# Two graph layers on one core: the bias add on another engine, and loads and stores at other places of a hand-ordered program

## The chip, the core and the metric

The kernel runs on one core of one Trainium2 chip. TensorE does the matrix products. VectorE (DVE), ScalarE (ACT) and GpSimd (POOL) work beside it. One queue, that of SyncE (SP), issues nearly all transfers between HBM and SBUF. The metric is the device time of one execution in microseconds (us).

## The reference, cut to what matters

```python
# x: 16 batches of 1024 x 128; adj: 1024 x 1024; all fp32
h = relu(layernorm(x))
x = x + (adj @ (h @ W0) + bias0)              # layer 0
h = relu(layernorm(x))
def step(h):                                  # layer 1: five steps
    m = adj @ h                               # in_matrix and out_matrix are both adj
    av = concatenate([m, m], axis=-1)
    u3 = h @ u3_w.T + u3_b
    z = sigmoid(av @ w3_w.T + w3_b + u3)
    r = sigmoid(av @ w4_w.T + w4_b + u3)
    hv = tanh(av @ w5_w.T + w5_b + (r * h) @ u5_w.T + u5_b)
    return (1 - z) * h + z * hv
x = x + step(step(step(step(step(h)))))
```

## The kernel before, in words

**Quads and stages.** The 16 batches are worked on in four quads of four. Layer 0's product with the adjacency matrix is done plainly for quads 0 and 1 (`aggregate_plainly`, L535; the trace calls its sums `pq_a`), and in layer 1's way for quads 2 and 3. While the plain products run, VectorE also makes sums of adjacency blocks (`right_sums`, L240), which are stored to HBM as `rd` and later streamed back.

**Layer 1.** Quads 0 and 1 take their steps in turn, then quads 2 and 3: (0,0), (1,0), (0,1), (1,1) and so on, where (q,n) is step n of quad q. The very last is (3,4). A step has two parts. In the *aggregation* (`aggregate`, L436) 49 small products of 256-blocks (7 x 7, a two-level scheme with fewer products than 8 x 8) give `mT`, adjacency times state. In the *gates* (`gates`, L711), first for the pair of batches A and then for the pair B, TensorE multiplies with the gate weights and VectorE updates the state `hT_all`.

**A product.** `multiply(i, p)` (L486) takes a left operand made by VectorE (`big`, `little`) and a right operand that is either resident or one of 12 slots of `ring`. ScalarE copies the result out of PSUM into `Z` or `taps`. After p = 3 and p = 4 VectorE adds these up (`Z<-Z,taps`), and after p = 4 it also adds a level into `mT`, for i = 4 three adds one after the other. After every second streamed product, `stream()` (L294) issues the load of a 512 KB pair that is used some ten products later (`ring<-rd`).

**Places.** What else is to be done is hung on places: `put(k, piece)` (L620) notes it, and `place(k)` (L623) runs the pieces of k. In an aggregation place k comes right after product k - 1. In the plain products there is a place every four matmuls. In the gates the places have names: `Ar0`-`Ar3`, `Az0`-`Az3`, `Br0`-`Bz3`. Each engine, and SP's queue, runs its own work in program order. A wait at the head of a queue holds all behind it.

**The pieces that matter here.**

- `bias(b)` (L647) adds layer 0's bias in place to the x tile of batch b, 128 partitions by 8 x 128 fp32. GpSimd does it. For quads 0 and 1 it stands at places of the two plain products, and for the others in `put_statistics` (L678), at 23 and 37 of a step.
- `TRANSPOSED` (L88): in the steps (1,0), (1,4) and (3,0) the four parked batches of a quad are loaded as 32 x 32 squares (`sqt<-ft`, `transposing`, L603) and turned by VectorE into `hT_all` (L613), two transposes each.
- After its gates each batch is turned back into squares (`squares_to_dram`, L576; `sq`) and stored (`fn<-sq`), for the next step to load in natural layout (`nat<-fn`).
- `output(b)` (L627) has three pieces: loads of `ho` (four transfers of 128 KB) and of `x1d` (512 KB), the add, and the store.
- The squares, `sqt`, `ho`, and the normalised batches `ha` and `hb` (written by `relu` of `put_statistics`) all share one pool `flip` of three buffers (L118). The tiles of x share a pool `pre` of four (L117).
- `po` (L651) multiplies by layer 0's weights and adds to x. Its PSUM bank comes from a pool of four, which the plain sums use as well (L123).

Of the kernel before, what the change touches and what calls it, by code (L numbers as in the profile page):

```python
# [93 lines left out]
def tile_two_gnn_layers(  # L94
# [9 lines left out]
    nc = tc.nc  # L104
    pin = tc.keep_in_program_order
# [6 lines left out]
    Q = 4  # L112
    quads = B // Q
# [11 lines left out]
    def dma(out, in_):  # L125
        pin(nc.sync.dma_start(out=out, in_=in_))

    def by_slots(ap):
        return ap.rearrange("(p c) d -> p c d", c=NC)

    def x_tile(b):
        return pre.tile([P, NC, D], F32, tag="xt", name=f"xt_{b}")

    def load_x(b, xt=None, parts=((0, NC),)):
        xt = xt if xt is not None else x_tile(b)
        for cs in parts:
            cs = slice(*cs)
            dma(xt[:, cs], by_slots(x[b])[:, cs])
        return xt
# [39 lines left out]
    xts = {0: load_x(0, parts=((0, 2), (2, CH), (CH, NC)))}  # L179
# [57 lines left out]
    def add(o, a, b):  # L237
        pin(nc.vector.tensor_add(o, a, b))  # L238
# [194 lines left out]
    def period(i):  # L433
        return 2 + 7 * i
# [132 lines left out]
    def flip_tile(nm):  # L567
        return flip.tile([P, NSQ, NC, SQ], F32, tag="sq", name=nm)
# [16 lines left out]
    def natural_from(blocks, hN):  # L585

        for k in range(NSQ):
            dma(by_blocks(hN, k), blocks[k])
# [31 lines left out]
    def put(k, *pieces):  # L620
        fixed.setdefault(k, []).extend(pieces)
# [5 lines left out]
    def output(b, blocks):  # L627
        box = {}

        def load():  # L630
            box["h"] = flip_tile(f"ho_{b}")
            natural_from(blocks, box["h"])
            box["x1"] = x_tile(f"1_{b}")
            dma(box["x1"], x1s[b])

        def rest():
            x1 = box["x1"].rearrange("p j (a e) -> p a j e", e=SQ)
            for g in range(NH):
                js = bass.ts(g, CH)
                add(x1[:, :, js], x1[:, :, js], box["h"][:, :, js])  # L640

        def store():
            dma(by_slots(out[b]), box["x1"])

        return load, rest, store

    def bias(b):  # L647
        both = gb.unsqueeze(1).to_broadcast([P, NC, D])
        pin(nc.gpsimd.tensor_add(xts[b], xts[b], both))

    def po(b, g):  # L651
        pt = ps_g.tile([P, CH, D], F32, tag="pg", name=f"po_{b}_{g}")
# [25 lines left out]
    def put_statistics(kind, first):  # L678

        rest = []  # L680
        for n, b in enumerate((first, first + 1)):
            box = {}

            def begin(b=b, box=box):
                box["n"] = Norm(xts[b], None, f"{kind}{b}")
                box["n"].statistics(range(CH))

            def relu(k, b=b, box=box):
                def run():
                    if k == 0:  # L690
                        box["n"].dst = flip_tile(f"h{kind}_{b}")
                    box["n"].relu(range(2 * k, 2 * k + 2))

                return run

            def done(b=b, box=box):
                (keep if kind == "a" else layer_1_input)(b, box["n"].dst)

            key = "AB"[n]
            put(f"{key}r3", begin)  # L700
            put(f"{key}z1", lambda box=box: box["n"].statistics(range(CH, NC)))
            put(f"{key}z3", lambda box=box: box["n"].scales(EVERY))
            rest.append((10, lambda box=box: box["n"].shift(EVERY)))
            rest += [(11 + 13 * n + 3 * k, relu(k)) for k in range(CH)]
            rest.append((22 + 14 * n, done))
            if kind == "a":
                rest.append((23 + 14 * n, lambda b=b: bias(b)))
        return rest


# [73 lines left out]
    def loads_of_next(source, places):  # L784

        for k, at in enumerate(places):
            put(at, lambda k=k: natural_from(source[k], nat[:, k]))

    def step(i, loads_at=(period(4), period(5), "Ar0", "Ar2"), early_places=GATE_PLACES):
        st = state[i]  # L790
        quad, n = st["quad"], st["step"]
        nm = f"{quad}_{n}"
        hT = [hT_all[:, i, k] for k in range(Q)]
        last = n == STEPS - 1
        final = last and quad == quads - 1
        other = state[1 - i]
        me = (quad, n)
        for k, piece in relus.pop("next", ()):
            put(k, piece)
        for b, k in LOADS.get(me, ()):  # L800
            put(k, lambda b=b: xts.update({b: load_x(b)}))
        if me in TRANSPOSED:
            q = TRANSPOSED[me]
            for k in range(Q):
                load, turn_it = transposing(q * Q + k, hT_all[:, q % 2, k])
                put((12, 16, 26, 30)[k], load)
                put((24, 28, 36, 40)[k], turn_it)
        if me in OUTPUTS:
            for k, piece in zip((16, 34, 38), outputs[OUTPUTS[me]]):
                put(k, piece)  # L810
        block = BLOCKS.get(me)

        source = h0_of(block) if block else other["blocks"]
        if final:
            st["x1"] = []

            def load_x1(k):
                x1 = x_tile(f"1_{quad * Q + k}")
                dma(x1, x1s[quad * Q + k])
                st["x1"].append(x1)  # L820

            for k in range(Q):
                for piece, at in zip(outputs[(quad - 1) * Q + k], (0, 13, 16)):
                    put(4 + 9 * k + at, piece)
            for k, at in enumerate((32, 42, "Ar0", "Ar3")):
                put(at, lambda k=k: load_x1(k))
        if source is not None:
            loads_of_next(source, loads_at)
        aggregate(nm, place)
        if me in NORMS:  # L830
            relus["next"] = put_statistics(*NORMS[me])
        if source is not None:
            for k, piece in zip(early_places, early_pieces(made[0])):
                put(k, piece)
        stored, ready = {}, {}

        def turn(first):
            def run(k):
                k += first
                stored[k] = Later(lambda n: ready[k][n])  # L840

                def squares():
                    store, ready[k] = squares_to_dram(hT[k], f"{nm}_{k}")
                    if k == Q - 1:
                        put(9, store)
                    else:
                        store()

                if k == Q - 1:
                    put(3, squares)  # L850
                else:
                    squares()

            return run

        for a, key in enumerate("AB"):
            pair = slice(2 * a, 2 * a + 2)
            if final and a == 1:
                for k, (load, rest) in enumerate(final_outputs(quad, st, stored)):
                    put(f"Br{2 * k}", load)  # L860
                    put(f"Bz{2 * k + 1}", rest)
            gates(
                [mT[:, 2 * a + k] for k in range(2)],
                hT[pair],
                f"{nm}{key}",
                key,
                turn(2 * a),
                finish=finish(quad, hT[pair], st) if final and a == 1 else None,
            )
        if final:  # L870
            st["quad"], st["blocks"] = None, None
            return
        st["step"] += 1
        st["blocks"] = [stored[k] for k in range(Q)]
        if last:
            outputs.update({quad * Q + k: output(quad * Q + k, stored[k]) for k in range(Q)})
            begin(i, quad + 2)
        if block:
            loads_of_next(other["blocks"], (period(3) + 4, period(4) + 4, period(5) + 2, period(6)))
            pieces = early_pieces(made[0] + 1)  # L880
            for k, piece in zip(BLOCK_PLACES, pieces):
                put(k, piece)
            aggregate(f"a{block}", place)
            for k in range(Q):
                for g in range(NH):
                    po(block * Q + k, g)
                    if 2 * k + g in (1, 2, 6, 7):
                        pieces[{1: 6, 2: 7, 6: 8, 7: 9}[2 * k + g]]()

    outputs = {}  # L890
# [21 lines left out]
    def h0_of(quad):  # L912
        return Later(lambda k: h0_blocks[quad * Q + k])
# [105 lines left out]
            (lambda: early(2 * Q - 1)) if b == Q else None,  # L1019
        )  # L1020
    for b in range(Q):
        put(9 + b // 2, lambda b=b: bias(b))
    for k in (3, 7, 8, 9, 10, 11, 12, 13, 14, 15):
        sums_at(k, 1)
    for b in range(Q):
# [39 lines left out]
    for k in range(Q):  # L1065
        b = Q + k
# [56 lines left out]
```

## Time and profile before

| what | value |
|---|---|
| time, median of 3 runs (lowest to highest) | 1807.7 us (1807.47 to 1808.23) |
| the profiled execution's own time | 1806.57 us |
| its span, first to last instruction | 1804.8 us |
| TensorE busy | 1774.4 us, 98% |
| VectorE busy | 1373.6 us, 76% |
| ScalarE busy | 900.1 us, 50% |
| GpSimd busy | 95.2 us, 5% |
| the 16 DMA engines, queue of SP | 68.4% |
| mean granted TensorE clock | 0.998 |

A row of a timeline gives the start in us, the duration, the engine, the line, what is written from what, the number of instructions merged, and in brackets how long the engine sat idle before and what ended that. A row of waits gives who waited for whom: us in total, times, longest.

### The profile page before, as it was taken

Reading aid. Unit: us, or ns where it says so; the run is one execution under the profiler, and the core shown is the slowest. Engines: PE = TensorE matmul, PEld = TensorE weight load, DVE = VectorE, ACT = ScalarE, POOL = GpSimd, SP = SyncE. Lnnn points to the kernel's source line nnn. Section 1 sums busy time; section 2 is a strip of 40 time slices with the busy share of each in tenths; the row PEclk is TensorE's granted clock in tenths of the full one; section 3 lists DMA queues with packets and bytes.
Section 4 is the critical chain, followed back from the end, with each engine's and each line's share of the span. In section 5 each row is a group of like instructions: output and inputs, shape, how many; then the busy total and the mean of one; then the engine's idle time right before and its main releaser. Section 6 shows DMA issues by size and latency. Waiting matters only on the chain.

```text
span 1804.8 us, 21485 instructions
## 1 busy us (share of the span) xinstructions
PE 1774.4 (98%) x6466; PEld 1208.6 (67%) x6466; DVE 1373.6 (76%) x2777; ACT 900.1 (50%) x1969; POOL 95.2 (5%) x57
## 2 busy tenths in 40 slices
PE   9999989999999999999999999999999999999998
PEld 4458576678685766758857667585766857667574
DVE  5758889677788697877787968777687777867776
ACT  5236555554555555644355554445445454444544
POOL 3331010100000001100000000000000000000000
PEclk9999999999999999999999999999999999999999
DMA  6298784759675957648849476594856749477493
GB/s 219 88 365 291 215 306 151 223 191 256 183 251 179 301 177 223 204 158 270 251 131 332 158 246 243 177 271 150 279 177 208 244 149 303 147 230 236 138 347 119
DMA packets 168866, 396.36 MB, mean 220 GB/s; under 512 B 18480, under 2 KB 86960, under 8 KB 168752
## 3 DMA queue, kind: packets, MB, share of 16 engines
q1 hardware_dynamic: 168752, 395.00, 68.4%
q8 instruction: 52, 0.85, 0.2%
q14 instruction: 62, 0.51, 0.1%
HBM read 314.18 MB, written 80.74 MB: 219 GB/s over the span
## 4 chain that ended last, share of the span: by engine, by line
PE 88%; DMA 5%; DVE 4%; issue 1%; POOL 1%; SPq 0%; ACT 0%; POOLq 0%; DVEq 0%; ACTq 0%
PE a L500 24%; PE c L500 12%; PE b L500 6%; PE pq_a L543 4%; PE a_a L500 3%; DMA ring<-rd 2%; PE pr_3B L720 2%; PE pr_2B L720 2%; PE pr_1B L720 2%; PE pr_4A L720 2%; PE pr_2A L720 2%; PE pr_1A L720 2%; PE pr_0A L720 2%; PE pr_3A L720 2%; PE pr_0B L720 2%; PE pr_4B L720 2%
## 5 line engine op out<-in xcount | busy, mean ns | idle before, releaser
L500 PE MATMUL a<-ring,big 128*128 128x256 f32 x1120 | 288.2, 380 | 4.4 <-DMA ring<-rd 4.4
L519 ACT COPY Z<-a 128x256 f32<-128x256 f32 x480 | 177.0, 371 | 209.1 <-PE a L500 202.7
L238 DVE TENSOR_TENSOR Z<-Z,taps 128x512 f32<-128x512 f32 (+1 forms) x264 | 157.5, 603 | 151.1 <-ACT taps L519 150.9
L500 PE MATMUL c<-ring,little 128*128 128x256 f32 x960 | 246.9, 380 | 5.5 <-ACT taps L519 3.3
L500 PEld LDWEIGHTS a<-ring,big 128*128 128x128 f32 x1120 | 212.8, 191 | 41.5 <-issue 11.8
L238 DVE TENSOR_TENSOR mT<-mT,Z 128x1024 f32<-128x1024 f32 x154 | 186.7, 1224 | 39.9 <-ACT Z L519 34.9
L500 PEld LDWEIGHTS c<-ring,little 128*128 128x128 f32 x960 | 182.4, 190 | 31.4 <-ACT taps L519 4.1
L519 ACT COPY taps<-c 128x256 f32<-128x256 f32 x280 | 103.6, 370 | 120.1 <-PE c L500 114.6
L500 PE MATMUL a<-ring,little 128*128 128x256 f32 x560 | 146.0, 384 | 6.5 <-DVE little L235 6.5
L500 PE MATMUL b<-ring,big 128*128 128x256 f32 x560 | 143.8, 380 | 0.0
L500 PE MATMUL a<-resident,little 128*128 128x256 f32 x560 | 143.8, 380 | 0.0
L500 PEld LDWEIGHTS a<-ring,little 128*128 128x128 f32 x560 | 105.6, 191 | 24.7 <-ACT taps L519 8.4
L500 PEld LDWEIGHTS b<-ring,big 128*128 128x128 f32 x560 | 106.7, 190 | 14.2
L500 PEld LDWEIGHTS a<-resident,little 128*128 128x128 f32 x560 | 106.7, 190 | 14.2
L581 DVE STREAM_TRANSPOSE sq<-hT_all 128x512 f32<-128x512 f32 x156 | 101.2, 687 | 0.0
L398 ACT COPY big<-nat 128x512 f32<-128x512 f32 x132 | 80.6, 614 | 0.0
L519 ACT COPY taps<-b 128x256 f32<-128x256 f32 x140 | 52.0, 371 | 55.5 <-PE b L500 55.0
L235 DVE TENSOR_TENSOR little<-little,big 128x256 f32<-128x256 f32 x154 | 65.4, 425 | 7.1 <-DVE little L238 0.5
L238 DVE TENSOR_TENSOR little<-big 128x256 f32<-128x256 f32 x154 | 64.2, 417 | 0.7 <-ACT big L398 0.7
L235 DVE TENSOR_TENSOR little<-big 128x256 f32<-128x256 f32 x154 | 64.2, 417 | 0.0
L235 DVE TENSOR_TENSOR little<-big,little 128x256 f32<-128x256 f32 x154 | 64.1, 416 | 0.0
L341 POOL TENSOR_TENSOR rstd_b<-ve_b,mhalf 128x8 f32<-128x8 f32 x16 | 27.5, 1717 | 550.0 <-DVE ve_b L340 536.6
(250 smaller groups left out, 2946.6 us busy)
## 6 DMA issues: line engine op xcount, KB each, us to landing
ring<-rd SPq DMA_DIRECT2D x440, 512.0 KB, 6.0
fn<-sq SPq DMA_DIRECT2D x78, 512.0 KB, 2.8
nat<-fn SPq DMA_DIRECT2D x256, 128.0 KB, 6.8
x1d<-xt SPq DMA_DIRECT2D x16, 512.0 KB, 5.6
sqt<-ft SPq DMA_DIRECT2D x16, 512.0 KB, 7.1
xt<-x1d SPq DMA_DIRECT2D x16, 512.0 KB, 7.0
xt<-in_x_dram SPq DMA_DIRECT2D x15, 512.0 KB, 5.3
ho<-fn SPq DMA_DIRECT2D x56, 128.0 KB, 6.3
```

Of the source, the lines that this page charges most:

```text
L235: pin(nc.vector.tensor_sub(o, a, b))
L238: pin(nc.vector.tensor_add(o, a, b))
L341: pin(nc.gpsimd.tensor_tensor(self.rstd[:, part], self.ve[:, part], mhalf[:, part], ALU.pow))
L398: return [lambda i=i: pin(nc.scalar.copy(made_of(k, i), part(a, b, i))) for i in range(2)]
L500: nc.tensor.matmul(bank, l, right[:, c, :], start=opens and c == 0, stop=c == SB - 1, skip_group_check=True,)
L519: pin(nc.scalar.copy(to, bank))
L543: nc.tensor.matmul(bank, hN[i][:, c, :], raw[c // SB][g][:, c % SB], start=c == 0, stop=c == NC - 1,)
L581: pin(nc.vector.transpose(squares_of_half(sq, g), transposed_half(hT, g)))
L720: nc.tensor.matmul(bank, w_sb[:, w, :], moving, start=start, stop=stop, skip_group_check=True)
```

## The change

Five edits:

1. VectorE does layer 0's bias add in place of GpSimd, and it stands at other places: 7 to 10 of the first plain product (before 9, 9, 10, 10), and 26 and 36 of a step (before 23 and 37). In the second plain product its places 6, 8, 10, 12 stay.
2. The parked batches of `TRANSPOSED` are loaded at 8, 18, 28, 38 and turned at 17, 27, 37, 47 (before 12, 16, 26, 30 and 24, 28, 36, 40).
3. The store of the squares of batch 2 of each quad is issued at place 4 of the next aggregation (before at once, in the gates). That of batch 3 stays at 9.
4. The pieces of the outputs of quad 2 in the last step stand earlier, and the first of them is loaded in step (2,4), at `Bz1`.
5. Of the four loads of the last quad's own x, the first two stand at 17 and 34 (before 32 and 42).

```diff
--- before.py
+++ after.py
@@ -646,7 +646,7 @@
 
     def bias(b):
         both = gb.unsqueeze(1).to_broadcast([P, NC, D])
-        pin(nc.gpsimd.tensor_add(xts[b], xts[b], both))
+        add(xts[b], xts[b], both)
 
     def po(b, g):
         pt = ps_g.tile([P, CH, D], F32, tag="pg", name=f"po_{b}_{g}")
@@ -704,7 +704,7 @@
             rest += [(11 + 13 * n + 3 * k, relu(k)) for k in range(CH)]
             rest.append((22 + 14 * n, done))
             if kind == "a":
-                rest.append((23 + 14 * n, lambda b=b: bias(b)))
+                rest.append((26 + 10 * n, lambda b=b: bias(b)))
         return rest
 
 
@@ -803,8 +803,8 @@
             q = TRANSPOSED[me]
             for k in range(Q):
                 load, turn_it = transposing(q * Q + k, hT_all[:, q % 2, k])
-                put((12, 16, 26, 30)[k], load)
-                put((24, 28, 36, 40)[k], turn_it)
+                put(8 + 10 * k, load)
+                put(17 + 10 * k, turn_it)
         if me in OUTPUTS:
             for k, piece in zip((16, 34, 38), outputs[OUTPUTS[me]]):
                 put(k, piece)
@@ -819,10 +819,11 @@
                 dma(x1, x1s[quad * Q + k])
                 st["x1"].append(x1)
 
-            for k in range(Q):
-                for piece, at in zip(outputs[(quad - 1) * Q + k], (0, 13, 16)):
-                    put(4 + 9 * k + at, piece)
-            for k, at in enumerate((32, 42, "Ar0", "Ar3")):
+            for k, places in enumerate(((None, 10, 13), (2, 18, 21), (15, 28, 31), (24, 40, 43))):
+                for piece, at in zip(outputs[(quad - 1) * Q + k], places):
+                    if at is not None:
+                        put(at, piece)
+            for k, at in enumerate((17, 34, "Ar0", "Ar3")):
                 put(at, lambda k=k: load_x1(k))
         if source is not None:
             loads_of_next(source, loads_at)
@@ -841,8 +842,8 @@
 
                 def squares():
                     store, ready[k] = squares_to_dram(hT[k], f"{nm}_{k}")
-                    if k == Q - 1:
-                        put(9, store)
+                    if k >= Q - 2:
+                        put({Q - 2: 4, Q - 1: 9}[k], store)
                     else:
                         store()
 
@@ -853,6 +854,10 @@
 
             return run
 
+        if last:
+            outputs.update({quad * Q + k: output(quad * Q + k, Later(lambda n, k=k: ready[k][n])) for k in range(Q)})
+            if quad == quads - 2:
+                put("Bz1", outputs[quad * Q][0])
         for a, key in enumerate("AB"):
             pair = slice(2 * a, 2 * a + 2)
             if final and a == 1:
@@ -873,7 +878,6 @@
         st["step"] += 1
         st["blocks"] = [stored[k] for k in range(Q)]
         if last:
-            outputs.update({quad * Q + k: output(quad * Q + k, stored[k]) for k in range(Q)})
             begin(i, quad + 2)
         if block:
             loads_of_next(other["blocks"], (period(3) + 4, period(4) + 4, period(5) + 2, period(6)))
@@ -1019,7 +1023,7 @@
             (lambda: early(2 * Q - 1)) if b == Q else None,
         )
     for b in range(Q):
-        put(9 + b // 2, lambda b=b: bias(b))
+        put(7 + b, lambda b=b: bias(b))
     for k in (3, 7, 8, 9, 10, 11, 12, 13, 14, 15):
         sums_at(k, 1)
     for b in range(Q):
```

## The prediction

> **What bounds the kernel now.** First the page's busy row and its chain that ended last: they name the engine that sets the end.
>
> ```profile
> PE 1774.4 (98%) x6466; PEld 1208.6 (67%) x6466; DVE 1373.6 (76%) x2777; ACT 900.1 (50%) x1969; POOL 95.2 (5%) x57
> ...
> PE 88%; DMA 5%; DVE 4%; issue 1%; POOL 1%; SPq 0%; ACT 0%; POOLq 0%; DVEq 0%; ACTq 0%
> ```
>
> TensorE carries 88% of the chain. An edit helps only where it shortens a wait of TensorE, and hurts only where it makes one. So I read TensorE's waits next, and where in time they lie.
>
> ```profile
> PE a L500 <- DVE little L235: 6.5, 6, 2.0
> PE a L500 <- DMA ring<-rd: 4.4, 4, 2.6
> PE po L655 <- DVE xt L238: 3.4, 1, 3.4
> PE c L500 <- ACT taps L519: 3.3, 2, 2.6
> PE c L500 <- DMA ring<-rd: 2.2, 2, 1.6
> ```
>
> Few and short. From TensorE's timeline I took each matmul's distance to the next above its form's median (its "excess"): 37.4 us in all, of 1804.8. That is all that any edit can win. A product takes 0.864 us and an undisturbed step 76.7 us. Then the timelines around the longest waits, VectorE, GpSimd and TensorE near 50 to 60 us first, ScalarE's and TensorE's late ones after.
>
> ```profile
> 46.43 2.31 DVE L346 SCALAR_TENSOR_TENSOR nmr_a<-mv_a,rstd_a 128x8 f32<-128x8 f32 x1 [0.39 <-POOL rstd_a L341]
> 49.37 5.49 DVE L235 TENSOR_TENSOR t<-ring,t 128x512 f32<-128x512 f32 x2
> 58.86 0.68 DVE L238 TENSOR_TENSOR xt<-po,xt 128x512 f32<-128x512 f32 x1
> ```
>
> ```profile
> 46.36 10.70 POOL L649 TENSOR_TENSOR xt<-xt,gb 128x1024 f32<-128x1024 f32 x4
> ```
>
> ```profile
> 59.60 1.16 PE L655 MATMUL po<-w_sb,mT 128*128 128x128 f32 x8 [3.42 <-DVE xt L238]
> ```
>
> While GpSimd's four bias adds run (46.4 to 57.1), VectorE's small op takes 2.31 us (0.17 elsewhere) and its 512-wide adds 2.7 each (0.68 elsewhere): the two engines shut each other out. `po`'s adder comes late, and TensorE waits 3.42.
>
> ```profile
> 241.81 0.88 ACT L359 ACTIVATE ha<-xt,nmr_a,rstd_a 128x128 f32<-128x128 f32 x2 [3.61 <-DMA h<-ha]
> ```
>
> ```profile
> 1746.38 1.25 PE L500 MATMUL a<-ring,big 128*128 128x256 f32 x4 [2.58 <-DMA ring<-rd]
> ```
>
> **The change part by part.** The sum is made against the profiled execution's 1806.57 us (the span and 1.8 around it). The median is 1.1 higher.
>
> *Bias on VectorE, first plain product.* Four adds 128x1024 come to VectorE. Its rows of that size cost 1224 ns, 1.13 from issue to issue: 4.5 us. Gone are the lock-outs: 2.1 on the small op, 4.1 on the two adds of 49.37, and some 2 on those after it, 8.4 us. So `po`'s add, at 58.86 before, comes at 54.5 to 55.2, and the excess of 3.58 us at 59.60 goes. The shift at 52.48 (TensorE waits 0.97 for ScalarE's `mT`) comes 0.3 earlier: 0.66 stays. After the wait TensorE's clock falls.
>
> ```profile
> 60.00:64.00 4.00, 4.00 (x12) 2.13 (x12) 3.96 (x8) 0.00 (x0) 0.00 (x0) 0.63 0.88 310
> 243.00:247.00 4.00, 4.00 (x19) 3.54 (x20) 1.41 (x3) 3.94 (x12) 0.00 (x0) 1.00 0.23 94
> 1748.00:1752.00 4.00, 4.00 (x14) 3.32 (x13) 3.90 (x4) 0.99 (x4) 0.00 (x0) 0.67 1.08 301
> ```
>
> In these windows the granted clock is the third column from the end. Four half-speed matmuls after 59.60 cost 1.8 us; that goes too. [...] The rows say that 2.58 us of waiting (1746.38) did it as well, at 1.5 us, and 2.61 (243.00, clock 1.00) did not. [...] by the rows it may cost 1.5 more. I take the rows, which matter in the last step below. Sum here: 3.6 + 1.8 + 0.3 = **5.7 won**.
>
> *Second plain product.* The x tiles that bias 4 to 7 change land late: GpSimd waits for them 21.1 us in all. These waits pass to VectorE. Queued behind each bias there are the `right_sums`, the turns of `sqt` and `po`'s adds. VectorE is busy 38.7 of the 65 us from 75 to 140. The last tile lands at about 128.1; bias 7 ends at 129.35, the turn at 130.6, `po`'s add at 131.3; TensorE wants that bank at 133.5. A margin of 2.2 us, so **0**; if that cover is gone, each us costs one. SP's queue behind it gets `sqt` and six ring loads some 4 us later, still in time.
>
> *Step (1,0): turns at 17, 27, 37, 47, loads at 8, 18, 28, 38.* The ScalarE row above: `relu` at place 24 waits 3.61 us for a buffer of `flip`, which the first turn frees only at 241.7. That turn is held by a GpSimd bias (235.6 to 238). TensorE loses 2.77 at 243.00. A turn at 17 frees it 6 us earlier: **2.77 won**. The other stall there (2.21 at 259.13, VectorE's `little` late in product 43) stays: a bias at 36 and a turn at 37 cost VectorE 1.13 + 1.25 ahead of it, as much as the lock-out and the turn at 36 before.
>
> [...] The edit shortens load to turn from 10 or 12 places to 9, 7.8 us. The row: `sqt` lands 3.5 to 11.0 us after its issue, 7.1 in the median. [...] by the row a median load is in time, and VectorE's idle 2.65 us around place 26 takes most of the rest. I take 0, bounds 0 and 3 in each of three steps.
>
> *Steps (0,1), (0,3), (1,3).* Each loses 1.03 at product 43: GpSimd's bias at 37 makes one `Z` add last 1.94 instead of 0.68, and the chain has little slack.
>
> ```profile
> 329.59 1.94 DVE L238 TENSOR_TENSOR Z<-Z,taps 128x512 f32<-128x512 f32 x1 [2.92 <-ACT taps L519]
> ```
>
> ```profile
> 610.25 0.69 DVE L238 TENSOR_TENSOR Z<-Z,taps 128x512 f32<-128x512 f32 x1 [2.92 <-ACT taps L519]
> ...
> 611.92 3.62 DVE L238 TENSOR_TENSOR mT<-mT,Z 128x1024 f32<-128x1024 f32 x3 [0.31 <-ACT Z L519]
> ```
>
> The second fence is the same place in a step without a bias: the slack is the 0.31. VectorE's own add at 36 stands in that chain: 1.13 - 0.31 = 0.8 plus its issue, 0.99. **0.1 won** in all three. The one at 26 lies in the idle 2.92.
>
> *Step (1,4).* ScalarE waits 1.69 for a turn (TensorE 0.86), and SP's queue stands blocked from 962 to 967.6 by a buffer that the turn at 28 frees, so ring loads come late (0.96). Both go. The turn at 37 follows the `mT` adds and takes the 0.31: 0.97 becomes 1.30. **1.5 won.** *Step (3,0)*: ring waits of 1.80 and 0.52 become 0.3 together, `little` 1.19 becomes 1.30: **1.9 won.**
>
> *Last step (3,4).* Its aggregation is bound by transfers, not by one wait:
>
> ```profile
> 1712.00:1760.00 48.00, 44.81 (x198) 38.29 (x197) 37.40 (x67) 19.56 (x51) 0.00 (x0) 0.96 0.97 328
> ```
>
> DMA is 0.97 busy. The bytes stay, except the first `ho` (four of 128 KB), which goes into (2,4). I put SP's queue through in issue order, with 1.25 us for 512 KB in a full queue and 3 for four strided 128 KB: before that gives 4.85 lost (measured 3.5 + 1.5 of clock), after 6.0, since the new order puts `ho`, `x1d` and stores ahead of more ring loads. Also `ho`, the squares and the next `ho` want four tiles of `flip`'s three at place 3, so VectorE waits there for a store, 3 us. **1.0 lost**, bounds 3 lost and 1.5 won.
>
> *Store of batch 2 at place 4.* SP stood waiting for these squares until some 1.4 us into each aggregation, and no ring load was late for it in an undisturbed step. Moved past three ring loads: **0**; if that cover is gone, 0.5 to 1 in a step.
>
> Sum: 5.7 + 2.8 + 0.1 + 1.5 + 1.9 - 1.0 = 11.0 won; 1795.6 for a profiled execution, **1797** for the median.
>
> **The rivals.** *(a) The waits change engine: slower.* The 21.1 us that GpSimd waits for x pass to VectorE and from there, over `po`'s banks, to TensorE. Price up to 21.1 - 11 = 10 more than before: 1817. It decides from a landing of the last tile later than about 130.1; the trace has 126.67. For it: VectorE is 76% busy and its queue is strict. Against: it has 26 idle us of 65 there. *(b) Loads too late for their turns, in three steps, 2.5 each:* 1804.5, no change. For it: 7.8 against 7.1. *(c) The place is not what it says:* `flip`'s buffer for the normalised batch is another one than the first turn frees, and ScalarE waits all the same. 2.77 + 0.86 are not won: 1800.7. *(d) The last step's queue jams* by 5 us instead of 1: 1801.
>
> **How the numbers follow.** 0.2%, 3.6 us, is about what a measurement of this kernel can tell from no change. The sum as it stands, 1791 to 1800: 0.66. (c) or (d), 1800 to 1804: 0.11. More than the sum, below 1791: 0.05. (b): 0.08. (a): 0.10. Faster is 0.66 + 0.11 + 0.05 = 0.82, same 0.08, slower 0.10. The range 1791 to 1805 leaves out (a), the best case and a little of (b).
>
> **What would show it.** No bias row on GpSimd, 16 more adds 128x1024 on VectorE. At 55 to 60 us no wait of `po` over 1 us and a clock of 1.00. In (1,0) no wait of ScalarE on `h<-ha`, and one stall of about 2 us at product 43 left. VectorE's waits for x in 95 to 130 up by some 15 us without any TensorE wait there. Product 43 of (0,1) still late by 1. In the last step some ring waits, 6 us together. Wrong would be: a TensorE wait over 2 us between 95 and 140, turns that wait for `sqt`, or ring waits in steps without any piece, from the store at place 4.

## The result, and the profile after

The changed kernel takes 1795.71 us in the median of six runs (1794.15 to 1800.02); the kernel before, measured with it, 1807.79. The ratio is 0.9933, with a 95% interval of 0.9917 to 0.9949: about 12 us faster, 1.3 below the forecast of 1797.

The profiled execution was the longest of the six, at 1800.02, 4.3 above the median, so its stages are compared one by one and not by their sum. First its busy row and the shares of its chain that ended last.

```profile
PE 1776.1 (99%) x6466; PEld 1208.7 (67%) x6466; DVE 1364.2 (76%) x2793; ACT 901.3 (50%) x1969; POOL 57.3 (3%) x41
...
PE 91%; DVE 4%; DMA 3%; issue 1%; ACT 1%; POOL 0%; SPq 0%; DVEq 0%; POOLq 0%; ACTq 0%
```

GpSimd has 16 instructions less and VectorE 16 more, yet VectorE's busy time fell by 9.4 us: the lock-outs had counted as its own work. (In the trace before, its instructions that overlap GpSimd's 16 adds last 24.9 us longer in all than the medians of their forms.) TensorE is still the bound. Its waits (us in total, times, longest):

```profile
PE a L500 <- DVE little L235: 9.0, 7, 2.8
...
PE a L500 <- DMA ring<-rd: 1.6, 1, 1.6
...
PE po L655 <- ACT mT L554: 0.7, 1, 0.7
PE a L500 <- ACT taps L519: 0.6, 1, 0.6
PE c L500 <- DMA ring<-rd: 0.6, 1, 0.6
```

The rows of `po <- DVE xt` and `c <- ACT taps` of before are gone, and the ring's two rows fell from 6.6 to 2.2. The row of `little` grew from 6.5 to 9.0, and its longest wait, 2.8, is new. In time order, VectorE's timeline of the start:

```profile
48.06 0.15 DVE L346 SCALAR_TENSOR_TENSOR nmr_a<-mv_a,rstd_a 128x8 f32<-128x8 f32 x1
48.14 1.21 DVE L238 TENSOR_TENSOR xt<-xt,gb 128x1024 f32<-128x1024 f32 x1
...
51.73 0.69 DVE L235 TENSOR_TENSOR t<-ring,t 128x512 f32<-128x512 f32 x1
...
54.26 0.68 DVE L238 TENSOR_TENSOR xt<-po,xt 128x512 f32<-128x512 f32 x1
```

The small op takes 0.15 in place of 2.31, the `t` add 0.69 in place of 2.7, and `po`'s adder comes at 54.26 in place of 58.86.

The last step has the new wait. In this order: two rows of SP's queue, one of VectorE, one of TensorE.

```profile
1705.17 1.85 SPq L126 DMA_DIRECT2D ho<-fn  x4
...
1708.07 0.38 SPq L126 DMA_DIRECT2D fn<-sq  x1
```

```profile
1715.31 1.30 DVE L581 STREAM_TRANSPOSE sq<-hT_all 128x512 f32<-128x512 f32 x2 [4.23 <-DMA fn<-sq]
```

```profile
1719.64 2.07 PE L500 MATMUL a<-ring,little 128*128 128x256 f32 x4 [2.80 <-DVE little L235]
```

The squares of batch 2 are stored at place 4, behind four `ho` loads, and land 7.2 us after their issue. VectorE wants that buffer for the squares of batch 3 and stands 4.23 us; `little` behind it is late, and TensorE waits 2.80. In windows of four microseconds the granted clock (third column from the end) shows what follows, first where `po` waited before, then behind the wait at 250 us in step (1,0), last behind the new one:

```profile
54.00:58.00 4.00, 4.00 (x16) 2.22 (x15) 3.96 (x8) 0.00 (x0) 0.00 (x0) 1.00 1.04 366
250.00:254.00 4.00, 3.78 (x11) 3.17 (x12) 2.19 (x6) 0.74 (x2) 0.00 (x0) 0.65 0.95 306
1720.00:1724.00 4.00, 4.00 (x10) 3.17 (x10) 3.90 (x9) 0.74 (x2) 0.00 (x0) 0.50 0.96 332
```

It is 1.00 in the first window, 0.65 in the second and 0.50 in the third.

Excess of TensorE by stage, in us, as the prediction defined it: 37.4 in all before, 30.9 after. The third number column is of other kernels below whose code in that stage is the changed one's.

| stage | before | after | same code elsewhere |
|---|---|---|---|
| first plain product, to 75 us | 11.4 | 5.5 | 5.8 (edit 1 alone) |
| second plain product | 0.9 | 0.9 | 0.9 |
| aggregation (1,0) | 5.3 | 3.9 | 2.3 and 2.3 |
| (0,1), (0,3), (1,3), each | 1.1 | 1.0 | 1.0 |
| (0,2) | 0.0 | 2.2 | 0.2 to 2.2 |
| (1,2) | 1.0 | 0.3 | 0.0 to 5.4 |
| (1,4) | 3.0 | 1.2 | 1.2 |
| aggregation (3,0) | 3.7 | 2.0 | 1.2 (three) to 2.8 |
| aggregation (3,4) | 5.3 | 6.8 | 6.8, 7.0 and 8.3 |
| last gates, after (3,4) | 2.8 | 4.4 | 2.7 to 4.6 |

What the last gates lose more is slow clock behind a wait of 2.07 us (granted clock 0.57 in the four microseconds from 1786.89); before has a wait of 1.98 at that place and a clock of 1.00 behind it.

### The profile page after: what moved, and what is told of

Same layout as the page of the kernel before. It is cut to its first block, busy times and chain, and to the rows that moved or that the text cites. A ratio compares the mean times of both kernels' runs of the same rounds, so it can differ in the third digit from the quotient of the medians.

```text
span 1798.2 us, 21453 instructions
## 1 busy us (share of the span) xinstructions
PE 1776.1 (99%) x6466; PEld 1208.7 (67%) x6466; DVE 1364.2 (76%) x2793; ACT 901.3 (50%) x1969; POOL 57.3 (3%) x41
## 4 chain that ended last, share of the span: by engine, by line
PE 91%; DVE 4%; DMA 3%; issue 1%; ACT 1%; POOL 0%; SPq 0%; DVEq 0%; POOLq 0%; ACTq 0%
PE a L500 25%; PE c L500 12%; PE b L500 6%; PE pq_a L543 4%; PE a_a L500 3%; PE pr_0A L720 2%; PE pr_3B L720 2%; PE pr_2A L720 2%; PE pr_1A L720 2%; PE pr_4A L720 2%; PE pr_3A L720 2%; PE pr_2B L720 2%; PE pr_1B L720 2%; PE pr_0B L720 2%; PE pr_4B L720 2%; PE pv_2A L720 2%
## 5 line engine op out<-in xcount | busy, mean ns | idle before, releaser
L238 DVE TENSOR_TENSOR Z<-Z,taps 128x512 f32<-128x512 f32 (+1 forms) x264 | 144.3, 553 | 143.4 <-ACT taps L519 143.4
L519 ACT COPY mT<-a 128x256 f32<-128x256 f32 x80 | 29.8, 373 | 47.5 <-PE a L500 47.5
```

The source lines that it names most:

```text
L519: pin(nc.scalar.copy(to, bank))
```

## The experiments

All are timed against the kernel before, which took 1809.42 us in the median beside experiments 1, 4, 5 and 6, 1809.59 beside 2, 7, 8 and 10, and 1808.55 beside 3, 9, 11 and 12; so the ratios compare better than the medians. "Excess" is read from each one's own trace.

**1. Edit 1 alone** (the bias on VectorE, at its new places).

> The kernel before with edit 1 alone (bias on VectorE, at 7 to 10 of the first plain product and at 26 and 36 of a step). Theory (lock-out): the wait at 60 us, its slow clock and 0.3 at 52 go (5.9), three stalls at product 43 fall from 1.03 to 0.91 (0.35), and in step (1,0) the first turn, which stood behind a locked VectorE op, comes 1 to 2 us sooner, so that ScalarE's wait for its buffer and TensorE's 2.77 shrink by as much: 7 to 8 less than before, 1800. Rival (the 21 us of waits for x pass to TensorE): 10 more than before. Rival (engine does not matter, only less waiting later): under 3 less.

Measured: 1800.06, ratio 0.9945 (0.9932 to 0.9957). First product 5.8 (before 11.4), the three biased steps 0.97 each, TensorE's waits in (1,0) 2.6 in place of 4.7. The second product lost 0.9, as before. The lock-out theory holds.

**2. The engine alone** (the places of before).

```diff
-        pin(nc.gpsimd.tensor_add(xts[b], xts[b], both))
+        add(xts[b], xts[b], both)
```

> The kernel before with VectorE adding the bias at the old places (9, 9, 10, 10 of the first plain product, 23 and 37 of a step): the engine alone, without the new places. Theory (the lock-outs cost, not the places): the wait at 60 us, and its slow clock, go as with edit 1 whole, 5 to 6 less there; product 43 of the steps with a bias no longer locked, 37 lies after the mT adds and costs 1.13 of VectorE there, about as much as the lock did. Total 6 to 9 less than before, like edit 1 whole (9.4 less). Rival (the new places matter as much): the wait at 60 us stays over 1.5 us, total under 4 less.

Measured: 1803.56, ratio 0.9960 (0.9946 to 0.9975). The first product's excess is 5.6: all of the start's gain comes from the engine, and TensorE's list of waits has no `po <- DVE xt`. The biased steps lose 1.17 each, 0.2 more than at 36. Against edit 1 whole the intervals overlap, so that the places of the steps are worth little or nothing.

**3. GpSimd at the new places** (the changed kernel, that line put back).

> The changed kernel with GpSimd adding the bias again, at the new places (7 to 10 of the first plain product, 26 and 36 of a step). Theory (the engine's lock-outs cost, not the places): TensorE waits 2.5 to 3.5 us for po near 60 us again and the clock falls after it; product 43 of (0,1), (0,3), (1,3) waits 0.9 or more; 5 to 7 more than the changed kernel, ratio to before 0.996 to 0.9975. Rival (four adds begun two places earlier are over in time): no wait of po, ratio 0.993.

Measured: 1800.86, ratio 0.9959 (0.9946 to 0.9973). GpSimd's and TensorE's timelines:

```profile
48.01 7.94 POOL L649 TENSOR_TENSOR xt<-xt,gb 128x1024 f32<-128x1024 f32 x3
```

```profile
54.12 4.54 PE L543 MATMUL pq_a<-Z,nat 128*128 128x512 f32 x6 [2.54 <-ACT mT L554]
```

The cost is about as expected (4.7 us by the ratios, 5 to 7 forecast), but at another place: the lock-out now delays VectorE's small op of the normalisation (`nmr_a`, 2.31 us at 48.07), ScalarE's normalisation and its copy to `mT` wait behind it, and the matrix product after it waits 2.54 us; its six matmuls take 4.54, where eight take 3.70 in the changed kernel. Excess 9.3. `po` itself is in time, so the place of the wait was forecast wrongly and its size rightly.

**4. Edit 2 alone** (turns and their loads).

> The kernel before with edit 2 alone (loads of parked batches at 8, 18, 28, 38, turns at 17, 27, 37, 47; GpSimd keeps the bias). Theory (a buffer of the shared pool comes free sooner): step (1,0) loses its 2.77 at 243 us, (1,4) falls from 3.1 to 1.3 and (3,0) from 3.6 to 2.0: 6 less, 1802; ScalarE's wait on h<-ha and on hT_all is gone. Rival (9 places are too short for the load): VectorE waits 2 to 3 us for sqt at the turns in each of the three steps, and the sum is within 2 of before.

Measured: 1800.86, ratio 0.9957 (0.9943 to 0.9971). Excess in (1,0) 2.4, (1,4) 1.2, (3,0) 1.2 (before 5.3, 3.0, 3.7): 7.2 won. VectorE's idle time in front of turns (us, times), first of the changed kernel, then of this one:

```profile
  DMA sqt<-ft: 13.2, 4
```

```profile
  DMA sqt<-ft: 23.4, 6
```

Of the 23.4, 8.5 lie in the second plain product, whose turns edit 2 leaves alone (before 7.3); 15.0 lie in the three steps, where before has 0.1. VectorE does wait for these loads, up to 5.8 us in (1,4) and 5.1 in (3,0), at the last turn; TensorE has then no wait on it. Both theories saw something true, and only the first one's reaches the time.

**5. Edits 4 and 5 alone** (outputs and own x in the last step).

> The kernel before with edits 4 and 5 alone (outputs of quad 2 earlier in the last step, first load in step (2,4), own x at 17 and 34); the squares of batch 2 are stored at once as before. Theory A (the queue of transfers sets it): ring waits in step (3,4) of 6 us against 5 before, total 1 more than before, 1809. Theory B (what the changed kernel lost there, a VectorE wait of 4.2 us for a buffer of the shared pool and 3 us of slow clock after it, comes from the store at place 4, not from these pieces): no such wait here, step (3,4) loses 1 to 2, total 3 to 4 less than before, 1804.

Measured: 1806.47, ratio 0.9984 (0.9975 to 0.9992): 1.4 to 4.5 won. VectorE has no wait at the squares of batch 3. Excess in (3,4) is 4.3, not 1 to 2. Theory B is right on where the wait comes from, and was too hopeful on the size.

**6. Edit 3 alone** (the store at place 4).

> The kernel before with edit 3 alone (squares of batch 2 stored at place 4 of the next aggregation, the last step too). Theory: no effect in undisturbed steps; same as before within 1 us. Rival (the store pushes ring loads back): the ring wait of 1.8 us that the changed kernel shows in step (0,2) at 535 us is there too, and others like it in more steps: 2 to 5 more than before.

Measured: 1809.97, ratio 0.9999 (0.9990 to 1.0008). (0,2) has no ring wait in this trace. No effect on the time to be seen.

**7. The changed kernel, squares of batch 2 at once in the last steps.**

```diff
-                    if k >= Q - 2:
+                    if k == Q - 1 or (k == Q - 2 and not last):
```

> The changed kernel, but in steps (q,4) the squares of batch 2 are stored at once again, so that no store at place 4 stands behind the output loads in the last step. Theory (VectorE's wait of 4.2 us at 1715 us came from that store, four tiles wanting three buffers): the wait and TensorE's 2.8 go, and the slow clock of 3 us with them; 3 to 6 less than the changed kernel, ratio to before 0.990 to 0.9915. Rival (the transfers set the step anyway): ring waits of the same 3 to 6 us come instead, ratio 0.993.

Measured: 1795.54, ratio 0.9914 (0.9893 to 0.9936). VectorE's timeline at the same instruction as at 1715.31 above:

```profile
1709.32 1.30 DVE L581 STREAM_TRANSPOSE sq<-hT_all 128x512 f32<-128x512 f32 x2
```

Its wait is gone. It takes two things together: VectorE waits there, 4.2 to 4.7 us, and TensorE 2.8 to 3.3 behind it, in the traces of all four kernels with the new order of the outputs and this store at place 4, and in none of the other ten. So the cause is shown. The gain is not: ring waits of 0.8 and 1.4 us come further on in the step, TensorE's waits there sum to 2.8 in place of 3.4, and what fell in this one profile is mostly slow clock (excess 6.8 to 3.8; mean granted clock 0.93 over 48 us of the step in the changed kernel, 1.00 here). By time it is 0.2 us by the medians and 3.4 by the ratios, whose intervals overlap. The fourteen traces, sorted by two things, have this excess in the last step (with slow clock that runs on into its gates):

| order of the outputs, store of batch 2 in the last step | excess of (3,4), each profile | mean |
|---|---|---|
| old, at once | 5.3, 8.2, 12.2, 5.6 | 7.8 |
| old, at place 4 | 10.0 | 10.0 |
| new, at once | 4.3, 3.8, 3.2, 5.8, 4.0 | 4.2 |
| new, at place 4 (the changed kernel) | 6.8, 6.8, 7.0, 8.3 | 7.2 |

**8. The second bias at 44 in place of 36.**

```diff
-                rest.append((26 + 10 * n, lambda b=b: bias(b)))
+                rest.append((26 + 18 * n, lambda b=b: bias(b)))
```

> The changed kernel with the second bias of a step at 44 instead of 36. Theory (VectorE's add stands in the chain of product 43 with 0.31 us of slack): the stalls of 0.9 us in (0,1), (0,3), (1,3) go, and the one of (1,0) falls from 2.1 to about 1.2[...]; 3.5 to 5.5 less than the changed kernel, ratio 0.9905 to 0.9915. Rival (the next chain, one period later, is as tight): a stall of the same size at product 46 to 49, ratio 0.993.

Measured: 1792.77, ratio 0.9901 (0.9877 to 0.9925). VectorE's timeline in (0,1), first of the changed kernel, then of this one:

```profile
323.31 1.22 DVE L238 TENSOR_TENSOR xt<-xt,gb 128x1024 f32<-128x1024 f32 x1
324.45 0.41 DVE L238 TENSOR_TENSOR Z<-Z,taps 128x256 f32<-128x256 f32 x1
324.97 3.62 DVE L238 TENSOR_TENSOR mT<-mT,Z 128x1024 f32<-128x1024 f32 x3
```

```profile
321.61 3.62 DVE L238 TENSOR_TENSOR mT<-mT,Z 128x1024 f32<-128x1024 f32 x3 [0.31 <-ACT Z L519]
...
327.22 1.22 DVE L238 TENSOR_TENSOR xt<-xt,gb 128x1024 f32<-128x1024 f32 x1
```

With the add ahead of the `mT` adds the slack of 0.31 is gone; behind them it is back, and the three steps lose 0.04 each in place of 0.97. (1,0) loses 1.3. By the ratios that is 5.8 us better than the changed kernel, by the medians 2.9, and the intervals overlap a little.

**9. Both of these, without other places of the turns.**

> The changed kernel with the squares of batch 2 of the steps (q,4) stored at once, and the second bias at 44: the combination without its new places of the turns. Theory (the two gains add up): 1791, ratio 0.9895; in (1,0) about 1.2 us lost, 1.2 each in (1,4) and (3,0), 3 to 4 in (3,4). Rival (the places of the turns were what brought the combination its 1788.6): no better than 1793.

Measured: 1789.53, ratio 0.9895 (0.9872 to 0.9918). (1,0), (1,4) and (3,0) lose 1.35, 1.22 and 1.22, as forecast, but (3,4) 5.8 and not 3 to 4. The two gains add up within the intervals.

**10. Both, and other places of the turns.**

```diff
-                put(8 + 10 * k, load)
-                put(17 + 10 * k, turn_it)
+                put((5, 16, 24, 33)[k], load)
+                put((14, 25, 33, 45)[k], turn_it)
```

> Both of the last two, and the parked batches loaded at 5, 16, 24, 33 and turned at 14, 25, 33, 45. Theory: no stall at product 43 is left (1.2 in (1,4), 1.2 in (3,0), the rest of (1,0) go as well), 10 to 13 less than the changed kernel, ratio 0.986 to 0.988. Rival (a turn at 33 or 45 is as badly placed as at 37, or its load is late): stalls of 1 to 2 us in (1,0), (1,4), (3,0), ratio 0.989 to 0.991.

Measured: 1788.56, ratio 0.9877 (0.9849 to 0.9904), the lowest median, clear of the changed kernel's interval and not of experiment 9's. The expectation came half true: (1,0) and (1,4) lose 0.1 and 0.4, but (3,0) 2.3, since the load for the turn at 33 lands 8.8 us after its issue; VectorE waits 3.6 for it, and TensorE 2.1. So the turns' new places are worth nothing on the whole that the times can tell.

**11. That, with edit 3 undone in every step.**

> The combination with edit 3 undone in every step (squares of batch 2 stored at once everywhere). Theory (edit 3 is worth nothing either way outside the last step): 1788.5 within 2. Rival (the store at place 4 brings the ring waits of 1.7 us in (0,2) and 3.4 us in (1,2)): these are gone, 1785. Other rival (edit 3 helps the gates, where SP stood waiting for the squares): 2 or more above.

Measured: 1789.05, ratio 0.9891 (0.9868 to 0.9913). Within 2, as the first theory had it. (0,2) loses 0.7 here and 2.2 in the combination, (1,2) 0.3 against 5.4; but experiment 8, which has edit 3, loses only 0.2 and 0.9 there. These ring waits of (0,2) and (1,2) come and go between kernels alike in them, and what sets them was not found. Over the fourteen traces (0,2) loses 1.2 in the mean in the eight kernels with edit 3 (0.0 to 2.2) and 0.3 in the six without (0.0 to 0.8), so that a part of edit 3 in it, some 1 us, is not ruled out.

**12. The last x tile of the second product loaded twice.**

```diff
+        if b == 3:
+            put(10, lambda: dma(xts[2 * Q - 1], by_slots(x[2 * Q - 1])))
```

> The changed kernel with the last x tile of the second plain product loaded twice, one load after the other, so that it lands about 4 us later (its values are the same). Theory (a margin of about 2 us lies between this tile's bias on VectorE and TensorE's next bank, and behind that each us costs one): VectorE's wait there grows from 7.4 to 11 us, TensorE loses about 2 us between 120 and 135, ratio 0.994 to 0.9945. Rival (VectorE catches up on other idle time, the margin is far wider): no wait of TensorE there, ratio 0.993. Other rival (what queues behind, turns and ring loads, is late as well): 4 or more lost, ratio 0.9955.

Measured: 1797.59, ratio 0.9937 (0.9917 to 0.9957). The first two rows are the changed kernel's bias adds in this window and the longest idle time in front of one, the other two this kernel's.

```profile
L238 DVE TENSOR_TENSOR xt<-xt,gb x4: 1224/1225/1226, 94.7 to 121.5; 128x1024 f32<-128x1024 f32 x4
...
  DMA xt<-in_x_dram: 7.4, 1
```

```profile
L238 DVE TENSOR_TENSOR xt<-xt,gb x4: 1225/1226/1226, 94.7 to 124.9; 128x1024 f32<-128x1024 f32 x4
...
  DMA xt<-in_x_dram: 10.1, 1
```

The last add comes 3.4 us later, 3.1 against TensorE's own products, which stand 0.3 later in this trace. TensorE doesn't wait: the product's excess stays 0.9. The margin is 3.1 us or more, not 2.2.

## Why the prediction was right, and where it was not

*First product:* 5.7 forecast, 5.9 in the trace. Experiments 2 and 3 show that it is the engine and not the place.

*Second product:* 0 forecast, 0 measured; VectorE's waits for x there are 17.6 us (about 15 forecast). The rival that ends slower had its mechanism right and its point of decision wrong: the margin is at least 0.9 us wider.

*(1,0):* 2.77 forecast. The wait went; in the profile 1.3 remains of that, since the other wait, forecast at about 2 and measured at 1.93 us, was followed by slow clock that cost 1.8 us. Experiments 7 and 12 have the same code there with a clock of 1.00, 3.0 won. Experiment 4 shows that edit 2 alone takes the first wait away.

*Biased steps:* 0.1 forecast, 0.3 measured; *(1,4)* 1.5 and 1.8; *(3,0)* 1.9 and 1.7. (SP's queue in (1,4) stood from 963.15 before, where its last row ends, and not from 962, to 967.62; the ring load behind went out at 968.03. Nothing in the sum hangs on it.)

*Loads and turns:* That load-to-turn of nine places is short was true for VectorE alone (up to 5.1 us in the changed kernel, outside the 3 that were allowed, which is about the longest landing of before, 11.0, less the 7.8 between). What the working left out is the way to the load: at the last turns of (1,4) and (3,0) the loads land 5.5 and 8.0 us after their issue, but SP's queue issues them some 8.7 and 5.6 us after TensorE is at place 38 (an estimate from 0.864 a product). TensorE did not wait for it: in (1,4) VectorE's last `little` of the aggregation is written at 972.1, before it stops for the turn at 974.6. For TensorE a late load cost something once, the 2.1 us of experiment 10, in the middle of an aggregation.

*Last step:* 1.0 lost forecast, 1.5 in the profile, but for another reason. The step that failed is the sum over SP's queue: the new order of the outputs was to cost more ring waits, 6 us together, and it saved some, 7.8 to 4.2 in the means above; the changed kernel's own profile has no ring wait in (3,4) at all. The four tiles for three buffers, put at 3 us of VectorE within this term, were the true loss: 4.2 us of VectorE, 2.8 of TensorE, in three of four traces with slow clock after, some 3 in the means. Two errors of opposite sign came near the right sum, which is luck. (The sum's times for transfers are estimates: 1.25 us for 512 KB is 419 GB/s, and before moved 414 from 1744 to 1748; its four `ho` loads from 1743.48 took 3.08 us to issue.)

*Additivity:* the single edits' ratios give 20.8 us together (1.15%), the change gave 12.1. A wait of 1.9 in (1,0) is in the gains of both edit 1 and edit 2, and some 3 us in the last step are lost only when edits 3 and 4 stand together. The rest, 3.8, is within the intervals.

*Signs of being wrong:* of the three that were named one came: turns that wait for `sqt`. A second came near: (0,2) has a ring wait of 1.63 us that no term of the sum had (2.1 lost, forecast 0). That step has other transfers beside the store at place 4, and experiments 6 and 11 leave the cause open. By stages the profile won 9.5 where the terms forecast 11.0, and 0.7 in (1,2); it lost the 2.1 of (0,2) and 1.6 in the last gates. The 12.1 of the time is from the medians, and this trace, the longest execution, does not split it.

*Clock:* the prediction took its price of a wait from the rows of before, and that held. Three waits of the changed kernel's profile, of 1.93, 2.80 and 2.07 us, have a granted clock of 0.62, 0.50 and 0.57 in the four microseconds behind them, and cost 1.8, 3.1 and 1.7 more.

## What to carry to other kernels

Where one engine's work stretches the other's, as GpSimd's 16 adds stretched VectorE's by 24.9 us here, a small job on the idle one is paid by the busy one: give it to the busy engine and price it there (here 1.13 us against some 2 for each neighbour held up). Put it behind, not ahead of, the chain with the least slack. When a store is moved later, count who holds that pool's buffers at that time: a store whose move alone shows no effect on the time can stop an engine once another edit fills the pool.

## What the runs showed of the hardware

*GpSimd and VectorE.* In the trace of before, 12 of GpSimd's 16 bias adds take 2.35 to 2.36 us, one 2.35 at the start (46.36), and the three behind it 2.79 to 2.88. While they run, VectorE's small op takes 2.31 (median of its form 0.16), `ve_b` at 100.18 takes 2.29 (0.17), and adds 128x512 between SBUF tiles take up to 2.83 (0.69). Not all of VectorE's work is held: five adds from `po` and two turns of `sqt` that overlap GpSimd's adds between 109 and 129 us take 0.65 to 0.71, as elsewhere.

*Waits and clock.* In the profiles of before and of the changed kernel TensorE has ten waits of over 1.6 us after the first 20. The clock is the mean that was granted in the four microseconds from the end of the wait; the cost is the excess of the matmuls behind it.

| kernel | wait ends at | wait | clock behind it | cost, us |
|---|---|---|---|---|
| before | 59.60 | 3.42 | 0.68 | 1.8 |
| before | 243.00 | 2.61 | 1.00 | 0 |
| before | 259.13 | 2.05 | 1.00 | 0 |
| before | 1123.86 | 1.63 | 1.00 | 0 |
| before | 1746.38 | 2.58 | 0.60 | 1.8 (the prediction has 1.5) |
| before | 1794.97 | 1.98 | 1.00 | 0 |
| after | 250.22 | 1.93 | 0.62 | 1.8 |
| after | 535.43 | 1.63 | 1.00 | 0 |
| after | 1719.64 | 2.80 | 0.50 | 3.1 |
| after | 1786.89 | 2.07 | 0.57 | 1.7 |

Over these ten that is 1.0 more a wait in the mean. The length alone does not tell them apart: 1.93 was followed by slow clock, 2.61 was not. Nor does the code. The wait of 1.93 to 1.94 us at product 43 of (1,0) stands in three profiles whose code is the same there; first two windows of the changed kernel, then of experiment 7, then of experiment 12 (TensorE's busy time stands behind the first comma, the clock third from the end):

```profile
248.00:252.00 4.00, 2.07 (x9) 1.53 (x8) 3.65 (x9) 0.74 (x2) 0.00 (x0) 0.90 1.01 311
252.00:256.00 4.00, 4.00 (x14) 3.30 (x13) 1.79 (x2) 1.11 (x3) 0.00 (x0) 0.68 1.01 391
```

```profile
248.00:252.00 4.00, 2.06 (x10) 1.51 (x10) 3.96 (x9) 0.84 (x3) 0.00 (x0) 1.00 1.02 315
252.00:256.00 4.00, 4.00 (x20) 3.53 (x19) 1.45 (x3) 1.64 (x5) 0.00 (x0) 1.00 0.99 373
```

```profile
248.00:252.00 4.00, 2.06 (x10) 1.53 (x9) 3.97 (x9) 0.84 (x3) 0.00 (x0) 1.00 1.09 301
252.00:256.00 4.00, 4.00 (x20) 3.52 (x19) 2.19 (x4) 1.59 (x5) 0.00 (x0) 1.00 1.02 410
```

It cost 1.8 us more in the first profile and nothing more in the other two. What decides it was not shown, so an excess read from a single profile can differ by that much without a cause in the code.
